# A position network with its 128 hidden channels sorted by sign: four keys a group, three partial sums added by one vector instruction and two accumulating transfers

## The chip, the cores and the metric

The kernel runs on one core of one Trainium2 chip. The metric is the device time of one execution in microseconds. Engines are called by their names in the profile: PE (matrix multiplication), PEld (PE's weight loads), DVE (vector), ACT (activation), POOL and SP (here mostly issuers of transfers), and the DMA engines behind the queues.

## The reference, cut to what matters

Four layers run one after the other on an image of 2 x 512 x 32 x 32. The change lies in the first, a deformable attention with 8 heads in each of 2 images, 1024 queries and 64 sampled keys. Each score gets a bias from a small network over the signed logarithm of the distance between query and key:

```python
pos = grid_q[:, :, None, :] - grid_kv[:, None, :, :]     # 16 heads x 1024 queries x 64 keys x 2
bias = jnp.sign(pos) * jnp.log1p(jnp.abs(pos))
bias = jax.nn.relu(bias @ cpb_w1 + cpb_b1)               # 2 -> 128
bias = jax.nn.relu(bias @ cpb_w2 + cpb_b2)               # 128 -> 128
bias = (bias @ cpb_w3 + cpb_b3)                          # 128 -> 1
sim = jnp.einsum('bhid,bhjd->bhij', qh, kh) + bias
attn = jax.nn.softmax(sim, axis=-1)
```

All data are float32. The rest of layer 0 (output projection with residual, MLP) and layers 1 to 3 are not edited.

## The kernel before, in words

`queries_keys_values` is the opening stage. It loads x into the tile `x_all`, makes q (kept padded in the tile `room`, as `q_pad`), runs the offset network (a depthwise convolution shared by PE, ACT and DVE, a gelu, a tanh), samples the keys and values, and leaves `kbd`, the keys in block form, and `val`.

`biased_scores` is the position network and more than half of the kernel. It loops over 8 head pairs p and, in each, over j = 0, 2, ... 30. Each step handles four groups t, and a group is two keys of one head (t // 2 chooses the head, t % 2 the half of its 64 keys). For one group:

- `hidden` makes one tile of 128 channels x 1024 queries for each key: an addition of two broadcast tables on DVE (L868, out of the `ab` tiles that `first_layer` loads by SP, L520, and scales on ACT, L533), then relu, in place, on ACT (L877) or, three times in sixteen, on DVE (L875). There are six such tiles.
- `second_layer` multiplies by the 128 x 128 weight in two halves of 64 channels. PE works in four column strips of 32, so that four matrix multiplications run side by side (L888). A half goes into one `ph` tile of two PSUM banks (three such tiles): strips 0 and 1 belong to the first key, 2 and 3 to the second.
- ACT evicts both halves with relu: `lo` (L898) with its bias, `hi` (L900) with a bias and a scale, the size of the last weight. DVE adds `lo` times a signed weight into `hi` (L901). This sum of 128 rows holds two keys of 64 rows each.
- `last_layer` (L909) multiplies four such sums (one j) by a 0/+1/-1 pattern into the `sim` tile (two PSUM banks), adding two keys of each group's 64 rows. It is placed one step later, behind the second group of the next j.

```python
lo = lows.tile([128, HW], F32, name="lo", tag="lo")
nc.scalar.activation(lo, phs[0], AF.Relu, bias=b2_lo)
hi = highs.tile([128, HW], F32, name="hi", tag="hi")
nc.scalar.activation(hi, phs[1], AF.Relu, bias=size_b, scale=size)
nc.vector.scalar_tensor_tensor(hi, lo, low_w, hi, ALU.mult, ALU.add)
```

At j = 16 of each p, `scores` adds q times k into the same `sim` banks (L921), and at the next p's start `store` copies `sim` to `simT` (L931). From p = 4 on, steps of the first image's softmax are woven in. At the last p, `q_pad` is no longer needed behind j = 16, and `load_weights` fills that tile with `out_w` and `mlp_w1` by SP (L321, L322). The output projection (L1055, L1067) and the MLP (L1127, L1116) follow. `Mlp` loads `mlp_w2` by SP (L217).

In float32 each matrix multiplication of the program shows up as two PE instructions. PE's order is the program's own (`manual_schedule`); the other engines' order comes from a scheduler, and each engine works its queue off in order. The compiler puts a semaphore wait where a tile is reused.

Of the kernel before, what the change touches and what calls it, by code (L numbers as in the profile page):

```python
# [16 lines left out]
B = 2  # L17
# [55 lines left out]
def constants():  # L73
    p = np.arange(128)
    px, py = (p % 32).astype(np.float32), (p // 32).astype(np.float32)
    neg_y = np.stack([-(py + 4.0 * c) for c in range(8)], axis=1).astype(np.float32)
    j = np.arange(64)
    gx, gy = (j % 8).astype(np.float32), (j // 8).astype(np.float32)

    gj = np.stack([gx, gy]).reshape(2, 1, 4, 16).repeat(16, axis=1)  # L80
    gj = gj.transpose(2, 0, 1, 3).reshape(128, 16)
    line = (2.0 * np.arange(32, dtype=np.float32) / np.float32(31) - 1.0).astype(np.float32)
    groups = np.zeros((128, 128), np.float32)
    for g in range(8):
        groups[16 * g : 16 * g + 16, 16 * g : 16 * g + 16] = 1.0 / 16

    y, x = np.divmod(np.arange(HW), 32)
    taps = np.zeros((HW, 9, 2), np.float32)
    for k in range(9):
        taps[:, k, 0] = y + k // 3 - 1  # L90
        taps[:, k, 1] = x + k % 3 - 1
    taps = taps.reshape(8, 128, 18).transpose(1, 0, 2).reshape(128, 144)
    parts = [
        ("ident", np.eye(128, dtype=np.float32)),
        ("groups", groups),
        ("minus", np.broadcast_to(np.array([0.0, -1.0], np.float32), (128, 2))),
        ("neg_xh", -px[:, None] - np.float32(0.5)),
        ("neg_yh", neg_y - np.float32(0.5)),
        ("gx", np.broadcast_to(gx, (128, 64))),
        ("gy", np.broadcast_to(gy, (128, 64))),  # L100
        ("gj", gj),
        ("line", np.broadcast_to(line, (128, 32))),
    ]
    packed, at = _pack(parts)
    return packed, at, taps


def layouts(i):
# [10 lines left out]
    for name in ("cpb_b2", "cpb_w3"):  # L119

        halves = np.asarray(i["L0_conv_" + name]).reshape(2, 64, 1)
        parts.append((name, np.concatenate([_twice(halves[0]), _twice(halves[1])], axis=1)))
# [20 lines left out]
    cst, cst_at, taps = constants()  # L143
# [8 lines left out]
    for h in range(2):  # L152
# [17 lines left out]
        "w2": np.asarray(i["L0_conv_cpb_w2"]),  # L170
# [24 lines left out]
class Net:  # L195
# [11 lines left out]
    def load_x(self):  # L207
        for b in range(B):
            for cc in range(CC):
                queue = (self.nc.sync, self.nc.gpsimd)[cc % 2]  # L210
                rows = slice(128 * cc, 128 * cc + 128)
                queue.dma_start(out=self.x[:, b, cc, :], in_=self.ins["x"][b, rows, :])
# [64 lines left out]
def layers(net, out):  # L277
# [12 lines left out]
    with ExitStack() as later:  # L290
# [12 lines left out]
        with ExitStack() as l0a:  # L303
# [8 lines left out]
            w2 = keys.tile([128, 128], F32, name="w2_t", tag="w2")  # L312
            first = net.pool(l0a, "cpb_ab", 4)
            parts = queries_keys_values(net, bn, simT, q_flat, q_pad, kbd, val, feat, first)
            nc.sync.dma_start(out=w2, in_=net.ins["w2"])

            def load_weights():
                t = new_room()
                w1 = t[:, : 4 * 2048].rearrange("p (k m) -> p k m", m=2048)
                out_w = t[:, 4 * 2048 :].rearrange("p (k m) -> p k m", m=C)  # L320
                nc.sync.dma_start(out=out_w, in_=net.ins["out_w"])  # L321
                nc.sync.dma_start(out=w1, in_=net.ins["mlp_w1"])  # L322
                return w1, out_w

            w1, out_w = biased_scores(
                net, q_pad, kbd, feat, w2, simT, first, parts, load_weights
            )
# [290 lines left out]
def queries_keys_values(net, bn, simT, q_flat, q_pad, kbd, val, feat, first):  # L618
# [5 lines left out]
    with ExitStack() as ctx:  # L624
# [3 lines left out]
        net.load_x()  # L628
# [11 lines left out]
        with ExitStack() as part:  # L640
# [33 lines left out]

            pd = bank("pd")
# [6 lines left out]
            nc.scalar.activation(g, g, AF.Gelu, bias=net.vec("odw_b"))  # L682

        with ExitStack() as part:
# [61 lines left out]

            for gt, name in grids:
# [58 lines left out]
            for w, out, factor in ((kw, kbd, 64**-0.5), (vw, val, 1.0)):  # L806
                for q in range(2):
# [15 lines left out]
                    )  # L823
    return done


def biased_scores(net, q_pad, kbd, feat, w2, simT, first, parts, load_weights):
# [12 lines left out]
    with ExitStack() as ctx:  # L840
        small = net.pool(ctx, "cpb_w", 1)
        hid1 = net.pool(ctx, "cpb_h1", 6)
        lows = net.pool(ctx, "cpb_lo", 2)
        highs = net.pool(ctx, "cpb_hi", 6)
        ps_h = net.psum(ctx, "cpb_ps_h", 3)
        ps_sim = net.psum(ctx, "cpb_ps_sim", 1)
        w3_lo, w3_hi = net.vec("cpb_w3", 0), net.vec("cpb_w3", 1)
        b2_lo, b2_hi = net.vec("cpb_b2", 0), net.vec("cpb_b2", 1)
        sign = small.tile([128, 1], F32, name="sign", tag="sign")
        nc.vector.tensor_scalar(sign, w3_hi, 0.0, 2.0, ALU.is_ge, ALU.mult)  # L850
        nc.vector.tensor_scalar(sign, sign, 1.0, None, ALU.subtract)
        size = small.tile([128, 1], F32, name="size", tag="size")
        nc.vector.tensor_tensor(size, w3_hi, sign, ALU.mult)
        size_b = small.tile([128, 1], F32, name="size_b", tag="size_b")
        nc.vector.tensor_tensor(size_b, size, b2_hi, ALU.mult)
        low_w = small.tile([128, 1], F32, name="low_w", tag="low_w")
        nc.vector.tensor_tensor(low_w, w3_lo, sign, ALU.mult)

        w3 = small.tile([128, 62], F32, name="w3", tag="w3")
        nc.vector.memset(w3, 0.0)  # L860
        nc.vector.tensor_copy(w3[0:64, 30:31], sign[0:64, :])
        nc.vector.tensor_copy(w3[64:128, 31:32], sign[64:128, :])

        def hidden(i, j, on_vector):
            at_x, at_y = parts[i, j % 32 // 16]
            k = 16 * (j // 32) + j % 16
            h1 = hid1.tile([128, HW], F32, name="h1", tag="h1")
            nc.vector.tensor_tensor(  # L868
                h1.rearrange("p (y x) -> p y x", x=32),
                at_x[:, k : k + 1, :].to_broadcast([128, 32, 32]),  # L870
                at_y[:, k, :].unsqueeze(2).to_broadcast([128, 32, 32]),
# [6 lines left out]
            return h1  # L878

        def second_layer(pair):  # L880

            phs = []
            for k in range(2):
                ph = ps_h.tile([128, HW], F32, name="ph", tag="ph")
                for n in range(2):
                    for t in range(4):
                        c0 = 64 * k + 32 * (t % 2)
                        nc.tensor.matmul(  # L888
                            ph[32 * t : 32 * t + 32, half(n)],
                            lhsT=w2[:, c0 : c0 + 32],  # L890
                            rhs=pair[t // 2][:, half(n)],
                            start=True,
                            stop=True,
                            skip_group_check=True,
                        )
                phs.append(ph)
            lo = lows.tile([128, HW], F32, name="lo", tag="lo")
            nc.scalar.activation(lo, phs[0], AF.Relu, bias=b2_lo)  # L898
            hi = highs.tile([128, HW], F32, name="hi", tag="hi")
            nc.scalar.activation(hi, phs[1], AF.Relu, bias=size_b, scale=size)  # L900
            nc.vector.scalar_tensor_tensor(hi, lo, low_w, hi, ALU.mult, ALU.add)  # L901
            return hi

        def last_layer(sim, j, sums):


            for n in range(2):
                for t in range(4):
                    nc.tensor.matmul(  # L909
                        sim[32 * t : 32 * t + 32, half(n)],  # L910
                        lhsT=w3[:, 30 - j : 62 - j],
                        rhs=sums[t][:, half(n)],
                        start=(j == 0),
                        stop=(j == 30),
                        skip_group_check=True,
                    )

        def scores(p, sim):
            for n in range(2):
                for t in range(2):  # L920
                    nc.tensor.matmul(  # L921
                        sim[64 * t : 64 * t + 64, half(n)].rearrange("p (y x) -> p y x", x=32),
                        lhsT=kbd[:, p, 64 * t : 64 * t + 64],
                        rhs=q_pad[:, p, 1 + 16 * n : 17 + 16 * n, 1:33],
                        start=False,
                        stop=False,
# [3 lines left out]
        def store(p, sim):  # L930
            nc.vector.tensor_scalar(simT[:, p, :], sim, net.vec("cpb_b3"), None, ALU.add)  # L931
# [16 lines left out]
        hidden_done = 0  # L948
        for p, j in [(p, j) for p in range(NP) for j in range(0, 32, 2)]:
            if j % 16 == 8:  # L950
                nxt = 2 * p + j // 16 + 1
                if nxt < 2 * NP:
                    parts.update(list(first_layer(net, first, feat, *divmod(nxt, 2)))[-1])
            sums = []
            for t in range(4):
                pair = []
                for k in range(2):
                    key = j + 32 * (t % 2) + k
                    pair.append(hidden(2 * p + t // 2, key, hidden_done % 16 in (3, 8, 13)))
                    hidden_done += 1  # L960
                sums.append(second_layer(pair))
                if t == 1 and pending is not None:
# [5 lines left out]
            elif j == 16:  # L968
                scores(p, sim)
                if p == NP - 1:  # L970
                    weights = load_weights()
            pending = (p, j, sums)
            if p >= CC and j % 8 == 4:
                next(beside, None)
        for _ in beside:
# [3 lines left out]
        return weights  # L979
# [1184 lines left out]
```

## Time and profile before

| | |
|---|---|
| three runs | 3830.58, 3833.95, 3833.63 us; median 3833.63 us |
| profiled execution | span 3835.8 us from the first to the last instruction; no other time is given for it, and it stands 2.2 us above the median of the runs |
| PE | 3739.0 us busy (97%), granted clock 0.992 in the mean |
| DVE, ACT | 2765.5 us (72%), 2566.4 us (67%) |
| POOL | 189.1 us (5%) |
| position network, from the first L888 to the last L909 | 86.6 to 2122.2 us |
| transfers | 168.57 MB, 44 GB/s in the mean |

How to read it: a group's line gives the source line, engine, operation, the tiles written and read, and how often; then the total busy time in us and the mean of one in ns; then the idle time before it and who ended it. Busy times of instructions that overlap are counted once in a total, so that a total can be less than count times mean. PE's matrix multiplications are pipelined and four strips overlap, so there the total divided by the count, not the mean, is the pace.

### The profile page before, as it was taken

To read this page: it belongs to the slowest core of one execution; us is meant where nothing else is said; L and a number is where in the kernel's file an instruction comes from. 1 tells how busy PE (TensorE), PEld (TensorE's weight loads), DVE (VectorE), ACT (ScalarE), POOL (GpSimd) and SP (SyncE) were. 2 spreads that over 40 slices of the span, in tenths; PEclk is the share of its full clock that TensorE was granted. 3 is DMA by queue.
4 is the path that set the end of the run, shared out by engine and by line. 5 is a ranking of instruction groups with operands and counts; after the bars stand their busy time and mean duration, and the time that the engine had idled before them with its cause. 6 is when DMAs were issued, how large, how long until landed. Compare 5 with 4: busy or idle time off the path is not lost. (4 is left out here: it accounts for less than half of the span.)

```text
span 3835.8 us, 59384 instructions
## 1 busy us (share of the span) xinstructions
PE 3739.0 (97%) x25356; PEld 1487.3 (39%) x25356; DVE 2765.5 (72%) x3242; ACT 2566.4 (67%) x2941; POOL 189.1 (5%) x180
## 2 busy tenths in 40 slices
PE   7999999999999999999999999999979999899999
PEld 4532222223222322232323444444434544455555
DVE  6999999999999999999999210411475472566565
ACT  7999999999999999999999221211123243345544
POOL 0000000000000000000000000000261150000000
PEclk9999999999999999999999999999999999999999
DMA  3000000000000000000000100112455481000000
GB/s 111 1 23 23 23 1 23 23 23 12 12 23 23 12 12 23 23 12 12 23 23 34 61 0 0 40 61 77 143 185 173 140 276 42 1 12 1 1 20 25
DMA packets 54459, 168.57 MB, mean 44 GB/s; under 512 B 4804, under 2 KB 10436, under 8 KB 51252
## 3 DMA queue, kind: packets, MB, share of 16 engines
q1 hardware_dynamic: 31556, 83.77, 6.2%
q0 software_dynamic: 21776, 79.14, 6.2%
q8 instruction: 200, 3.28, 0.4%
q10 hardware_dynamic: 864, 1.86, 0.2%
q14 instruction: 63, 0.52, 0.0%
HBM read 156.11 MB, written 8.65 MB: 43 GB/s over the span
## 5 line engine op out<-in xcount | busy, mean ns | idle before, releaser
L888 PE MATMUL ph<-h,w_t 128*32 128x512 f32 x16384 | 1808.0, 593 | 15.7 <-ACT lo L898 6.5
L868 DVE TENSOR_TENSOR h<-ab 128x1024 f32<-128x1024 f32 x1024 | 1206.0, 1219 | 67.2 <-PE ph L888 66.2
L888 PEld LDWEIGHTS ph<-h,w_t 128*32 128x32 f32 x16384 | 547.6, 110 | 1239.9 <-issue 1017.2
L877 ACT ACTIVATE h<-h 128x1024 f32<-128x1024 f32 x832 | 872.1, 1067 | 45.6 <-DVE h L868 42.9
L901 DVE SCALAR_TENSOR_TENSOR hi<-lo,low_w,hi 128x1024 f32<-128x1024 f32 x512 | 654.8, 1279 | 31.6 <-ACT hi L900 30.3
L900 ACT ACTIVATE hi<-ph,size_b,size 128x1024 f32<-128x1024 f32 x512 | 621.3, 1214 | 16.7 <-PE ph L888 12.5
L898 ACT ACTIVATE lo<-ph,vec_t 128x1024 f32<-128x1024 f32 x512 | 571.8, 1117 | 5.8 <-PE ph L888 5.4
L2086 ACT ACTIVATE e<-pl,m 128x1024 f32<-128x1024 f32 x128 | 143.6, 1122 | 228.9 <-DVE m L2078 228.9
L1567 PE MATMUL po<-fold,turned 128*128 128x512 f32 x576 | 266.1, 606 | 3.2 <-DVE dfacc L1575 2.9
L2078 DVE TENSOR_REDUCE m<-pl 128x1 f32<-128x1024 f32 x128 | 150.7, 1219 | 147.2 <-PE pl L1988 147.2
L1135 ACT ACTIVATE h<-ph,vec_t 128x512 f32<-128x512 f32 x64 | 44.0, 687 | 312.0 <-PE ph L1127 311.5
L909 PE MATMUL sim<-hi,w 128*32 128x512 f32 x2048 | 251.0, 592 | 0.0
L1127 PE MATMUL ph<-xn,room 128*128 128x512 f32 x512 | 230.9, 594 | 0.0
L1116 PE MATMUL acc<-h,mlp_w_t 128*128 128x512 f32 x512 | 229.8, 592 | 0.0
L1514 DVE SCALAR_TENSOR_TENSOR sum<-got,wts,sum 128x256 f32<-128x256 f32 x432 | 184.4, 478 | 48.8 <-ACT sum L1510 46.4
L1490 POOL DMA_INDIRECT got<-table,idx x144 | 175.0, 1215 | 554.9 <-DVE sum L1514 268.0
L2040 PE MATMUL pt<-cst_t,e 128*128 128x128 f32 x1024 | 149.3, 279 | 6.6 <-ACT aT L2051 4.0
L2040 PEld LDWEIGHTS pt<-cst_t,e 128*128 128x128 f32 x1024 | 118.6, 142 | 93.6 <-issue 61.3
L1567 PEld LDWEIGHTS po<-fold,turned 128*128 128x128 f32 x576 | 106.6, 195 | 112.4 <-issue 107.4
L1116 PEld LDWEIGHTS acc<-h,mlp_w_t 128*128 128x128 f32 x512 | 97.3, 190 | 122.5 <-issue 122.0
L1127 PEld LDWEIGHTS ph<-xn,room 128*128 128x128 f32 x512 | 96.6, 191 | 117.7 <-issue 117.1
L1541 ACT COPY turned<-pt 128x512 f32<-128x512 f32 x72 | 41.9, 582 | 143.8 <-PE pt L1535 143.6
(250 smaller groups left out, 2711.6 us busy)
## 6 DMA issues: line engine op xcount, KB each, us to landing
ab<-feat_d SPq DMA_DIRECT2D x64, 512.0 KB, 4.0
room<-in_dc_w_dram SPq DMA_DIRECT2D x9, 1024.0 KB, 4.8
dc_w_t<-in_dc_w_dram SPq DMA_DIRECT2D x5, 1024.0 KB, 5.3
room<-in_mlp_w_dram SPq DMA_DIRECT2D x1, 4096.0 KB, 15.6
mlp_w_t<-in_mlp_w_dram SPq DMA_DIRECT2D x1, 4096.0 KB, 12.5
dc_w_t<-in_dc_w_dram SPq DMA_DIRECT2D x8, 512.0 KB, 5.0
w_qkv_t<-in_w_qkv_dram SPq DMA_DIRECT2D x3, 1024.0 KB, 8.6
out_dram<-x_all SPq DMA_DIRECT2D x12, 256.0 KB, 2.0
```

The source lines that it names most:

```text
L868: nc.vector.tensor_tensor(h1.rearrange("p (y x) -> p y x", x=32), at_x[:, k : k + 1, :].to_broadcast([128, 32, 32]), at_y[:, k, :].unsquee ...
L877: nc.scalar.activation(h1, h1, AF.Relu)
L888: nc.tensor.matmul(ph[32 * t : 32 * t + 32, half(n)], lhsT=w2[:, c0 : c0 + 32], rhs=pair[t // 2][:, half(n)], start=True, stop=True, skip_ ...
L898: nc.scalar.activation(lo, phs[0], AF.Relu, bias=b2_lo)
L900: nc.scalar.activation(hi, phs[1], AF.Relu, bias=size_b, scale=size)
L901: nc.vector.scalar_tensor_tensor(hi, lo, low_w, hi, ALU.mult, ALU.add)
L909: nc.tensor.matmul(sim[32 * t : 32 * t + 32, half(n)], lhsT=w3[:, 30 - j : 62 - j], rhs=sums[t][:, half(n)], start=(j == 0), stop=(j == 30 ...
L1116: nc.tensor.matmul(accs[oc], lhsT=self.w2[:, m, 128 * oc : 128 * oc + 128], rhs=hs[m], start=(m == 0), stop=(m == 15),)
L1127: nc.tensor.matmul(ph, lhsT=self.w1[:, k, 128 * m : 128 * m + 128], rhs=xn[:, k, :], start=(k == 0), stop=(k == CC - 1),)
L1514: nc.vector.scalar_tensor_tensor(t[:, q, :], g[:, s, :], w, t[:, q, :], ALU.mult, ALU.add)
L1567: nc.tensor.matmul(self.out, lhsT=turned[:, at : at + 128], rhs=self.folded.w[k][:, i, :], start=(k == 0 and i == 0), stop=(k == 8 and i = ...
L2040: nc.tensor.transpose(pt[:, 128 * c : 128 * c + 128], e[:, 128 * k : 128 * k + 128], ident)
```

## The change

The 128 channels of the second layer are sorted on the chip by the sign of their last weight, so that one lane of 32 rows has the same sign in the last three quarters; the first quarter may have lanes whose sign differs. The size of each last weight is multiplied into the second layer's weights and bias. A group is then four keys, one for each strip of 32 rows, and the 128 channels are done in four quarters. `Order` makes the sorted weights in the opening stage (`ranks`, `places`, `put`: small instructions on one column, two loads, seven small matrix multiplications).

- `hidden` makes two keys in one instruction of 128 x 2048. Its tiles are nine pairs: five in `room`, whose `q_pad` is no longer needed, and four in `x_all`. Seven relus in sixteen are on DVE.
- `second_layer`: four quarters into four `ph` tiles; ACT evicts all four with relu and a bias. DVE adds the first to the second (`lo`, one buffer). The third and fourth (`r2`, two buffers; `r3`, three) are added by transfers with `accum_op=ALU.add`, issued by POOL from SBUF to SBUF; the fourth's is issued one group later, behind the next group's third.
- `last_layer` runs for every fourth key instead of every second, behind the third group of the next step. Eight buffers hold the totals, as against six.
- q times k is done for all p at the end of the opening stage and copied to `simT` by DVE and ACT; `store` adds to it.
- x is loaded again by SP: the first image and `out_w` at the last p's j = 24, when three of the nine pairs are given up, the second image at the end; `mlp_w1` comes in four parts at the end.

```diff
+    def put(self, bank):
+        net, nc = self.net, self.net.nc
+        pw, pb = bank("pw2"), bank("pb2")
+        nc.tensor.matmul(pw[:, :128].rearrange("p (q l) -> p q l", l=32),
+            lhsT=self.turned, rhs=self.spread[:, :, 0, :], start=True, stop=True)
...
+            order.places(ranks)
...
+            order.put(bank)
...
+            for p in range(NP):
+                for n in range(2):
+                    pq = bank("pqk")
+                    for t in range(2):
+                        nc.tensor.matmul(
+                            pq[64 * t : 64 * t + 64, :].rearrange("p (y x) -> p y x", x=32),
+                            lhsT=kbd[:, p, 64 * t : 64 * t + 64],
+                            rhs=q_pad[:, p, 1 + 16 * n : 17 + 16 * n, 1:33],
...
+                    (nc.vector.tensor_copy, nc.scalar.copy)[n](simT[:, p, half(n)], pq)
...
-        hid1 = net.pool(ctx, "cpb_h1", 6)
-        lows = net.pool(ctx, "cpb_lo", 2)
-        highs = net.pool(ctx, "cpb_hi", 6)
+        lows = net.pool(ctx, "cpb_lo", 1)
+        thirds = net.pool(ctx, "cpb_r2", 2)
+        fourths = net.pool(ctx, "cpb_r3", 3)
+        highs = net.pool(ctx, "cpb_hi", 8)
...
             nc.vector.tensor_tensor(
-                h1.rearrange("p (y x) -> p y x", x=32),
-                at_x[:, k : k + 1, :].to_broadcast([128, 32, 32]),
-                at_y[:, k, :].unsqueeze(2).to_broadcast([128, 32, 32]),
+                h1.rearrange("p k (y x) -> p k y x", x=32),
+                at_x[:, k : k + 2, :].unsqueeze(2).to_broadcast([128, 2, 32, 32]),
+                at_y[:, k : k + 2, :].unsqueeze(3).to_broadcast([128, 2, 32, 32]),
                 ALU.add,
             )
...
+        def quarter(quad, q):
+            ph = ps_h.tile([128, HW], F32, name="ph", tag="ph")
+            for n in range(2):
+                for t in range(4):
+                    nc.tensor.matmul(
+                        ph[32 * t : 32 * t + 32, half(n)],
+                        lhsT=order.w2[:, 32 * q : 32 * q + 32],
+                        rhs=quad[t][:, half(n)],
...
+        def second_layer(quad, late):
+            r0 = rectified(quarter(quad, 0), 0, lows, "lo")
+            total = rectified(quarter(quad, 1), 1, highs, "hi")
+            nc.vector.scalar_tensor_tensor(total, r0, order.low, total, ALU.mult, ALU.add)
+            r2 = rectified(quarter(quad, 2), 2, thirds, "r2")
+            r3 = rectified(quarter(quad, 3), 3, fourths, "r3")
+            nc.gpsimd.dma_start(out=total, in_=r2, accum_op=ALU.add)
+            flush(late)
+            late.append((total, r3))
+            return total
+
+        def flush(late):
+            for total, more in late:
+                nc.gpsimd.dma_start(out=total, in_=more, accum_op=ALU.add)
+            late.clear()
...
         def store(p, sim):
-            nc.vector.tensor_scalar(simT[:, p, :], sim, net.vec("cpb_b3"), None, ALU.add)
+            nc.vector.scalar_tensor_tensor(
+                simT[:, p, :], sim, net.vec("cpb_b3"), simT[:, p, :], ALU.add, ALU.add
+            )
...
-        for p, j in [(p, j) for p in range(NP) for j in range(0, 32, 2)]:
+        rooms = room.rearrange("p (n k i) -> p n k i", k=2, i=HW)
+        tiles = [rooms[:, n] for n in range(5)]
+        tiles += [net.x[:, b, c : c + 2, :] for b in range(B) for c in range(0, CC, 2)]
+        slots = list(range(9))
+        for p, j in [(p, j) for p in range(NP) for j in range(0, 32, 4)]:
...
+            if (p, j) == (NP - 1, 24):
+                slots = [at for at in slots if at not in (4, 5, 6)]
+                load_out()
+                net.load_x(0, [nc.sync])
...
-                    pair.append(hidden(2 * p + t // 2, key, hidden_done % 16 in (3, 8, 13)))
+                    on_vector = pairs_done * 7 % 16 < 7
+                    quad += hidden(2 * p + t // 2, key, tiles[slots[0]], on_vector)
...
-                if t == 1 and pending is not None:
+                if t == 2 and pending is not None:
                     last_layer(sim, *pending[1:])
...
+        net.load_x(1, [nc.sync])
+        flush(late)
```

## The prediction

> **What bounds the kernel now.** I read first the slices of the profile's page, to find the stage, then the costliest groups of instructions, then the busy time of each engine in stretches of the stage, then the rows of transfers that POOL issues, and last the order of time around the stage's two ends.
>
> ```profile
> PE   7999999999999999999999999999979999899999
> DVE  6999999999999999999999210411475472566565
> ACT  7999999999999999999999221211123243345544
> DMA  3000000000000000000000100112455481000000
> ```
>
> For the first 22 of 40 slices PE, DVE and ACT are all above 90%, while the DMA engines do next to nothing. That is the position network, from 86.6 to 2122.2 us: 2035.6 us, or 7.95 us for each of 256 sets of four keys.
>
> ```profile
> L888 PE MATMUL ph<-h,w_t 128*32 128x512 f32 x16384 | 1808.0, 593 | 15.7 <-ACT lo L898 6.5
> L868 DVE TENSOR_TENSOR h<-ab 128x1024 f32<-128x1024 f32 x1024 | 1206.0, 1219 | 67.2 <-PE ph L888 66.2
> L877 ACT ACTIVATE h<-h 128x1024 f32<-128x1024 f32 x832 | 872.1, 1067 | 45.6 <-DVE h L868 42.9
> L901 DVE SCALAR_TENSOR_TENSOR hi<-lo,low_w,hi 128x1024 f32<-128x1024 f32 x512 | 654.8, 1279 | 31.6 <-ACT hi L900 30.3
> L900 ACT ACTIVATE hi<-ph,size_b,size 128x1024 f32<-128x1024 f32 x512 | 621.3, 1214 | 16.7 <-PE ph L888 12.5
> L898 ACT ACTIVATE lo<-ph,vec_t 128x1024 f32<-128x1024 f32 x512 | 571.8, 1117 | 5.8 <-PE ph L888 5.4
> L909 PE MATMUL sim<-hi,w 128*32 128x512 f32 x2048 | 251.0, 592 | 0.0
> ```
>
> PE waits 15.7 us in all for anyone; DVE and ACT mostly wait for PE or for each other. The stretch 300 to 600 us settles it (PE, PEld, DVE, ACT, POOL busy, then PE's clock, DMA share, GB/s):
>
> ```profile
> 300.00:600.00 300.00, 298.18 (x2756) 88.18 (x2752) 284.77 (x259) 292.56 (x287) 0.00 (x0) 1.00 0.07 22
> ```
>
> PE is the bound at 99.4%, at full clock. ACT at 97.5% and DVE at 94.9% are close behind, so a gain on PE alone would be lost to ACT within 2%; all three have to come down together. The pace is 300 / 2756 = 0.1089 us for one matrix multiplication.
>
> **The change part by part.** *PE.* The second layer keeps its 16384 instructions. The last layer has one sum for four keys instead of two: 1024 of 2048 fall away, 1024 x 0.1089 = 111.5 us. The 64 of q times k (L921, 15.5 us busy) move ahead of the stage. The stage's PE pace becomes (2035.6 - 111.5 - 15.5) / 256 = 7.46 us a group of four keys.
>
> *ACT.* A group has four evictions with a bias, like L898: 4 x 1.117 = 4.47. Relu of a pair: L898 against its 512-wide kin L1135 (0.687) gives 0.43 for 512 elements, so 1.067 + 0.86 = 1.93; nine sixteenths of two pairs are 1.125 x 1.93 = 2.17. The tables cost 64 x 1.219 / 256 = 0.30. Sum 6.94 by means; neighbours overlap by some 5% in the rows of before, so about 6.5 of 7.46. *DVE.* Two additions of a pair (1.219 at 1024 and 0.689 at 512 give 1.06 for 1024 more, so 2.28): 4.56. Relu of a pair (0.686 at 1024, 0.42 at 512, so 1.21) 0.875 times: 1.06. One L901: 1.28. `store` 0.04. Sum 6.94, about 6.6 with overlap. Both fall from 95% and more to about 88% of PE's time. That cover is what makes PE's gain count: if it were gone, DVE without overlap would still be under 7.46.
>
> *The transfers.* Here lies the risk. Nothing in the trace accumulates. The nearest rows are the gathers of layer 1, which POOL issues too, 512 KB each; the view of transfers in the stretch 2460 to 3170 us gives the software queue's packets, MB and share of the engines, and the median us to landing:
>
> ```profile
> q0 software_dynamic: 20896, 76.03, 32.3%
> ...
> got<-table,idx POOLq DMA_INDIRECT x144, 5.3
> ```
>
> So 76.03 MB took 0.323 x 710 = 229 us of all sixteen engines, 332 GB/s, 1.58 us for 512 KB, with 5.3 us from issue to landing and, by the median of L1490, 0.94 us of POOL. Lower bound of an accumulating one: a copy's 1.58 us. Upper bound: it lands before the next begins, 5.3 us. I take 3.2 us, twice a copy, because the sum has two sources to read; it is nearer to the copy's row, because gathers overlap in flight (58 of them, 307 us of landing times, lie between 2700 and 2900 us). Two a group are 6.4 us, the `ab` loads (64 x 1.58 / 256) 0.4: 6.8 of 7.46 us, hidden with a tenth to spare. The limit is (7.46 - 0.39) / 2 = 3.53 us; above it the transfers set the pace, and at 3.75 us the whole gain is gone.
>
> The Trainium skill ("Collectives: The Full Stack", section "The bandwidth ceiling: the fold count and why AG ≠ RS ≠ AR") holds that adding in the transfer is slow through its two source reads and not through the addition, and gives 31 GB/s an engine halved. By that rule sixteen engines would add 250 GB/s, an estimate from that page, 2.1 us a transfer, and the sum would be the same, with more room; no run here shows it.
>
> The added waits: ACT's `r2` waits for the transfer two groups back, `r3` for the one three back that was issued a group late, and behind them stand all evictions, so PE. With 5.3 + 1.6 us to land, `r2`'s is done some 7 us after issue, and ACT needs it after 14.9; the totals must be ready 2 groups and more after the last issue. So nothing waits as long as the rate holds. POOL's order is third of this group, then fourth of the last; 2 x 0.94 us of POOL is a quarter of a group.
>
> DVE and POOL can also hold each other up. L650, a `tensor_scalar` of 128x1024, takes 0.80 us seven times, and 1.72 us the one time that POOL's memsets L634 and L635 run beside it, at 6.3 us. No row shows the same beside an issue of POOL. If every one of the 224 relus on DVE were held for one issue, 0.94 us, DVE would go from 6.6 to 7.4 us a group, just short of PE. The Trainium skill ("SBUF — State Buffer", section "Who interferes with whom") makes it a rule, and one that speaks against this change: a vector instruction that uses both of DVE's port pairs and POOL's descriptor writing lock each other out for their whole length.
>
> *Opening stage.* 32 small DVE instructions come between the convolution's L591, which runs back to back there. Such ones (L853 to L862) start 0.07 to 0.16 us apart: 2.2 to 5.1, I take 3.5. The ten behind the gelu fit into DVE's wait of 3.18 us for `nt`. Moving q times k puts 15.5 us ahead of the first L888, but PE stood idle 3.4 + 0.5 us there for the first `hidden`, and that is now filled: -3.9. The 16 copies (0.69, 0.58 us) run on two engines beside it. The small matrix multiplications lie in PE's idle 6.3 us before L788. Emptying PSUM for the next pool: +1.
>
> *End of the stage.* Before, L900, L901 and L909 followed the last L888; DVE's part was 1.28 us:
>
> ```profile
> 2117.11 1.21 ACT L900 ACTIVATE hi<-ph,size_b,size 128x1024 f32<-128x1024 f32 x1 [0.60 <-PE ph L888]
> ...
> 2118.34 1.28 DVE L901 SCALAR_TENSOR_TENSOR hi<-lo,low_w,hi 128x1024 f32<-128x1024 f32 x1 [2.15 <-ACT hi L900]
> ```
>
> Now two transfers stand there one behind the other, each 3.9 (the fastest gather) to 7 us, the first starting one quarter, 1.74 us, earlier: 7.8 to 14, less 1.74 and 1.28, so +4.8 to +11, and SP's reloads run at that moment: +9. The reloads themselves: `mlp_w1` landed in 15.6 us before, and the first L1127 comes at 2155.9, 38 us after the last L888; the second image is needed later still, and `mlp_w2` (12.5 us) behind it at 2162.4. 10 MB at 332 GB/s are 32 us, so 6 us of cover remain; without it the MLP would start late by as much. At j = 24 `out_w` and an image, 3 MB, hold the transfers up by 9 us once, less than the 7.5 us of slack plus what the buffers give.
>
> *Sum.* -111.5 + 3.5 - 3.9 + 1 + 9 = -102, and I expect PE's 0.6% of idling in the stage, 12 us, to halve with the other engines' slack: -6. 3835.8 - 108 = 3728 in the profile's terms; the span is 2.2 us over the median, so 3725.
>
> **The rivals.** *The transfers pace the stage* (slower). Place: POOL's queue and the sixteen engines; it decides from 3.53 us on. If an addition costs three passes (two reads, one write, 4.75 us), a group is 2 x 4.75 + 0.4 = 9.9 us, and the time 3725 + 256 x 2.44 = 4350 us; at 5.3 us, 4630. For it: no row of accumulation, and a margin of a tenth. Against it: the copy's 1.58 us lies far below.
>
> *Just at the edge.* Transfers of 3.6 to 3.75 us, or DVE held by POOL without its overlap (6.94 + 0.82 = 7.76 us): 20 to 90 us back, 3745 to 3815.
>
> *It does not do what it says.* If PE's pace were set by ACT's chain rather than by its own count, taking 1024 away would bring little; PE's wait of 15.7 us speaks against it. Time: about 3833.
>
> **How the numbers follow.** Forecast 0.66, with its own range 3690 to 3760: all ends at their best (-111.5 - 12 - 3.9 + 2.2 + 4.8, and PE at the 0.1075 us that L909's rows of 16 show) to all at their worst and 20 us of the reloads uncovered. Edge 0.12, faster still. No change 0.03. Paced by transfers 0.19. A difference of 0.2%, 7.7 us, is about what a measurement of this kernel can tell. Faster 0.78, same 0.03, slower 0.19. The range runs from 3690 to 3850; left out are nearly all of the slower case and a little at the bottom.
>
> **What would show it.** Right: L909's successor x1024, PE above 98% in the stage at about 7.4 us a group, DMA share there 0.8 to 0.95, DVE and ACT below 92%, 4 to 11 us of PE idle at the stage's end. Wrong: PE's idle time ended by ACT evictions that in turn wait for DMA, a DMA share of 1 with POOL waiting for its own transfers, or a relu on DVE far above 1.2 us.

## The result, and the profile after

| | before | after |
|---|---|---|
| median (range) | 3833.1 us (3830.6 to 3834.0, 4 runs) | 3993.6 us (3985.4 to 3997.4, 4 runs) |
| profiled execution's span | 3835.8 us | 3989.8 us |
| PE, DVE, ACT, POOL busy | 97%, 72%, 67%, 5% | 92%, 65%, 57%, 16% |

The changed kernel is slower by 160 us: ratio 1.0414, 95% interval 1.0400 to 1.0429. The forecast of 3725 us, and its range, were wrong.

The slices of the changed kernel's page:

```profile
PE   7998899989899999899998799999988999999999
DVE  7987788778778888788887211320366374466665
ACT  7887777777787777777876321021113233245544
DMA  3577777776777677767777700012345473000000
```

In the position network PE has fallen from solid nines to a mixture with eights, and DVE and ACT to seven and eight tenths. DMA stands at seven tenths, neither idle nor full. No engine is the bound. The costliest groups say what they wait for:

```profile
L1017 PE MATMUL ph<-room,w_t 128*32 128x512 f32 x9184 | 1255.8, 597 | 108.9 <-ACT r L1029 78.8
L1017 PE MATMUL ph<-x_all,w_t 128*32 128x512 f32 x7200 | 1030.1, 596 | 84.7 <-ACT r L1029 67.1
L1029 ACT ACTIVATE r<-ph,bias 128x1024 f32<-128x1024 f32 x512 | 550.5, 1110 | 409.9 <-DMA hi<-r 392.2
...
L1046 POOL DMA_DIRECT2D hi<-r x256 | 219.6, 858 | 1697.1 <-DVE hi L1036 438.4
L1039 POOL DMA_DIRECT2D hi<-r x256 | 307.1, 1200 | 80.8 <-ACT r L1029 78.2
```

PE waits 193.6 us, 145.9 of them for evictions of `r2` and `r3`, and these in turn wait 392 us for transfers (`hi<-r`) to give their buffers back. I call the third quarter's transfer A2 (L1039) and the fourth's A3 (L1046). Of POOL's two rows, A3's has nearly all of the idle time in front of it, 1697 us against 81. The stretch 300 to 600 us (PE, PEld, DVE, ACT, POOL busy, PE's clock, DMA share, GB/s), and then the view of transfers in it (packets, MB, share of the engines; below it KB each):

```profile
300.00:600.00 300.00, 264.50 (x2380) 73.33 (x2376) 235.82 (x136) 226.78 (x189) 61.03 (x70) 1.00 0.72 141
```

```profile
q0 software_dynamic: 10126, 36.83, 65.6%
...
hi<-r POOLq DMA_DIRECT2D x70, 512.0 KB
```

70 transfers took 0.656 x 300 = 197 us of all sixteen engines, **2.81 us each**, less than the 3.2 that I took and than my limit of 3.53. So their price alone doesn't explain the loss. POOL's order of time does:

```profile
1003.53 0.85 POOL L1046 DMA_DIRECT2D hi<-r  x1 [10.99 <-DVE x_all L1008]
1004.07 1.21 POOL L1039 DMA_DIRECT2D hi<-r  x1
1011.22 0.86 POOL L1046 DMA_DIRECT2D hi<-r  x1 [5.94 <-ACT hi L1029]
1011.75 1.21 POOL L1039 DMA_DIRECT2D hi<-r  x1
1020.14 0.85 POOL L1046 DMA_DIRECT2D hi<-r  x1 [7.18 <-DVE hi L1036]
```

A3 goes first and A2 0.54 us behind it. Then POOL stands for 6 to 11 us, and a waiting A3 opens the next pair. The brackets name whatever ended last by the profile, often an instruction that writes nothing an A3 reads (`x_all`, for one); 279.7 us, in 44 waits, are put down to the transfers themselves. The engines work in bursts between:

```profile
1004.80:1009.90 5.10, 3.31 (x32) 0.59 (x24) 0.00 (x0) 5.10 (x5) 0.47 (x1) 1.00 1.04 197
1009.90:1012.50 2.60, 2.27 (x24) 0.78 (x28) 1.28 (x2) 2.54 (x4) 1.28 (x2) 1.00 0.13 24
```

5.1 us with all of them at work without pause (share 1.04), then 2.6 nearly empty. The trace doesn't say which group an A3 belongs to, since buffer numbers are left out, but the instruction list of the built kernel does. POOL's queue holds:

```
L1039 hi_892<-r2_904
L1046 hi_892<-r3_915
L1039 hi_942<-r2_954
L1046 hi_942<-r3_965
```

The source writes A2 of a group and then A3 of the group before (`flush(late)`). The scheduler, free to order POOL, put A3 right behind the A2 of its *own* group. The first rows of the stage show the same: when the first A3 comes, one A2 alone has gone, and the A3 waits for a transfer.

```profile
118.46 0.91 POOL L1039 DMA_DIRECT2D hi<-r  x1 [75.40 <-ACT r L1029]
123.59 0.87 POOL L1046 DMA_DIRECT2D hi<-r  x1 [4.23 <-DMA hi<-r]
124.89 0.86 POOL L1039 DMA_DIRECT2D hi<-r  x1 [0.43 <-issue]
```

A3 must wait for A2 to land, since both add into one tile, and it waits at the head of POOL's queue, so the next group's A2 stands behind it. That makes one round a group. The shorter of the two rounds shown above, from the A3 at 1003.53 to the one at 1011.22, takes 7.7 us: 0.5 between the two issues, 2 x 2.81 of data, and a remainder of some 1.6 (an estimate) for the way from issue to start and from landing to the next issue. The next one takes 8.9. Over the stage the median of 255 rounds is 8.1 us, and the 28 in which loads of the `ab` tiles are asked for take 9.8 in the mean. The stage, from PE's first L1017 at 107.0 to its last at 2246.7, took 8.36 us a group where PE needs under 7.46.

### The profile page after: what moved, and what is told of

Same layout as the page of the kernel before. It is cut to its first block, busy times and chain, and to the rows that moved or that the text cites. A ratio compares the mean times of both kernels' runs of the same rounds, so it can differ in the third digit from the quotient of the medians.

```text
span 3989.8 us, 57248 instructions
## 1 busy us (share of the span) xinstructions
PE 3688.4 (92%) x24346; PEld 1430.2 (36%) x24346; DVE 2584.3 (65%) x2562; ACT 2265.8 (57%) x2406; POOL 638.7 (16%) x692
## 5 line engine op out<-in xcount | busy, mean ns | idle before, releaser
L1017 PE MATMUL ph<-room,w_t 128*32 128x512 f32 x9184 | 1255.8, 597 | 108.9 <-ACT r L1029 78.8
L1017 PE MATMUL ph<-x_all,w_t 128*32 128x512 f32 x7200 | 1030.1, 596 | 84.7 <-ACT r L1029 67.1
L1029 ACT ACTIVATE r<-ph,bias 128x1024 f32<-128x1024 f32 x512 | 550.5, 1110 | 409.9 <-DMA hi<-r 392.2
L1001 DVE TENSOR_TENSOR room<-ab 128x2048 f32<-128x2048 f32 x287 | 646.9, 2285 | 7.3 <-PE ph L1017 7.1
L1017 PEld LDWEIGHTS ph<-room,w_t 128*32 128x32 f32 x9184 | 340.3, 110 | 835.6 <-issue 549.5
L1036 DVE SCALAR_TENSOR_TENSOR hi<-lo,low,hi 128x1024 f32<-128x1024 f32 x256 | 328.5, 1283 | 392.2 <-ACT hi L1029 391.9
L1001 DVE TENSOR_TENSOR x_all<-ab 128x2048 f32<-128x2048 f32 x225 | 507.7, 2285 | 6.9 <-PE ph L1017 6.8
L1017 PEld LDWEIGHTS ph<-x_all,w_t 128*32 128x32 f32 x7200 | 274.4, 110 | 655.2 <-issue 428.1
L1046 POOL DMA_DIRECT2D hi<-r x256 | 219.6, 858 | 1697.1 <-DVE hi L1036 438.4
L1039 POOL DMA_DIRECT2D hi<-r x256 | 307.1, 1200 | 80.8 <-ACT r L1029 78.2
L1010 ACT ACTIVATE room<-room 128x2048 f32<-128x2048 f32 x163 | 311.7, 1912 | 11.2 <-DVE room L1001 10.6
L1029 ACT ACTIVATE lo<-ph,bias 128x1024 f32<-128x1024 f32 x256 | 285.1, 1114 | 50.2 <-PE ph L1017 49.1
L1029 ACT ACTIVATE hi<-ph,bias 128x1024 f32<-128x1024 f32 x256 | 285.3, 1114 | 13.6 <-PE ph L1017 13.1
L1010 ACT ACTIVATE x_all<-x_all 128x2048 f32<-128x2048 f32 x125 | 239.0, 1912 | 4.7 <-DVE x_all L1001 4.4
```

Source lines behind the costliest of these rows:

```text
L1001: nc.vector.tensor_tensor(h1.rearrange("p k (y x) -> p k y x", x=32), at_x[:, k : k + 2, :].unsqueeze(2).to_broadcast([128, 2, 32, 32]), a ...
L1010: nc.scalar.activation(h1, h1, AF.Relu)
L1017: nc.tensor.matmul(ph[32 * t : 32 * t + 32, half(n)], lhsT=order.w2[:, 32 * q : 32 * q + 32], rhs=quad[t][:, half(n)], start=True, stop=Tr ...
L1029: nc.scalar.activation(t, ph, AF.Relu, bias=order.bias[:, q : q + 1])
L1036: nc.vector.scalar_tensor_tensor(total, r0, order.low, total, ALU.mult, ALU.add)
L1039: nc.gpsimd.dma_start(out=total, in_=r2, accum_op=ALU.add)
```

## The experiments

In kernels that put POOL in order the source lines are two higher (L1031 for L1029, L1041 and L1048 for A2 and A3). Ratios are to the kernel before, in the same set.

**First set: order, buffers, bytes, addition.**

```diff
-l0a.enter_context(net.tc.manual_schedule(engines={mybir.EngineType.PE}))
+l0a.enter_context(net.tc.manual_schedule(engines={mybir.EngineType.PE, mybir.EngineType.Pool}))
```

> Edit: POOL also follows the written order in the stage, so that A2 of a group (the third quarter's transfer) is issued ahead of A3 of the group before; nothing else changes. Order theory (POOL's built queue puts A3 of a group right behind its own A2, so one round of issue, start, data and landing is paid for each group, 8.1 to 8.5 us against PE's 7.46): the groups fall back to PE's pace, 256 x (8.4 - 7.5) = 230 us are gone, about 3763 us, with 3745 to 3790 as its bounds; PE's busy share in the window 300 to 600 us rises from 88% to 98% or more. Rate rival (two transfers of 2.81 us and their start and landing fill the DMA engines' time whatever the order): 3960 to 4000 us, and DMA bursts still follow each other with the same gaps. Buffer rival (two r2 buffers stall ACT): no change either, since the buffers are as they were.

Measured: 3850.1 us (3848.7 to 3854.7), ratio 1.0052 [1.0035, 1.0069]. POOL's first rows in the stage now have two A2 ahead of the first A3:

```profile
116.07 0.91 POOL L1041 DMA_DIRECT2D hi<-r  x1 [73.00 <-ACT r L1031]
122.52 0.86 POOL L1041 DMA_DIRECT2D hi<-r  x1 [5.54 <-DVE hi L1038]
123.07 1.20 POOL L1048 DMA_DIRECT2D hi<-r  x1
```

143 us are gone, so the order is a cause and the rate rival falls. But 230 were expected, PE is busy 281 of the 300 us from 300 on and not 98%, and the kernel is still no faster than before.

```diff
-thirds = net.pool(ctx, "cpb_r2", 2)
-fourths = net.pool(ctx, "cpb_r3", 3)
+thirds = net.pool(ctx, "cpb_r2", 3)
+fourths = net.pool(ctx, "cpb_r3", 2)
```

> Edit: three r2 buffers and two r3 buffers in place of two and three, POOL's queue as in the changed kernel. Buffer rival (ACT's third-quarter eviction waits for a buffer that the transfer two groups back still reads; that is where the trace puts ACT's 392 us of idle time): most of 240 us is gone, 3760 to 3850 us. Order theory (ACT's wait is only the place where POOL's round shows): 3980 to 4000 us, no change, and the wait moves to another instruction.

Measured: 3995.8 us (3988.6 to 4005.8), ratio 1.0423 [1.0405, 1.0440]: no change. ACT's wait (473 us here, at the same evictions) shows where POOL's round is felt, and a buffer more for `r2`, at `r3`'s cost, does not help. More buffers in all were not tried.

```diff
-nc.gpsimd.dma_start(out=total, in_=r2, accum_op=ALU.add)
+nc.gpsimd.dma_start(out=total[:, :512], in_=r2[:, :512], accum_op=ALU.add)
```

and the same for `r3`:

> Edit: both transfers of a group carry columns 0 to 511 only, so half of the additions are left out; POOL's queue as in the changed kernel. Order theory with a round made of bytes: the round of 8.1 us loses 2 x 1.4 = 2.8 us and becomes 5.3, below PE's 7.46, so 3750 to 3790 us. Latency rival (the round is mostly fixed start and landing, the bytes count little): the round stays over 7.46 us, 3880 us or more.

Measured: 3731.2 us, ratio 0.9736 [0.9720, 0.9752].

```diff
-nc.gpsimd.dma_start(out=total, in_=r2, accum_op=ALU.add)
+nc.gpsimd.dma_start(out=total, in_=r2)
```

and the same for `r3`:

> Edit: the two transfers of a group copy instead of adding, so two of the three additions are left out; POOL's queue as in the changed kernel. Order theory with the accumulation's price in it: a copy of this size takes about 1.6 of the engines' us against 2.81, the round falls from 8.1 to 5.6 us, below PE's 7.46: 3750 to 3790 us. Rival (an accumulating transfer costs no more than a copy from SBUF to SBUF, 2.8 us each): 3970 to 4000 us.

Measured: 3732.0 us, ratio 0.9736 [0.9720, 0.9752]. Both came out below the bounds expected. The software queue's row between 300 and 600 us, first of the half-width run (82 transfers), then of the copies (82):

```profile
q0 software_dynamic: 11885, 21.66, 42.2%
```

```profile
q0 software_dynamic: 11819, 43.00, 35.8%
```

A half-width addition takes 0.422 x 300 / 82 = 1.54 us of the engines, a full copy 1.31, against 2.81 for a full addition. By the sum above the round is then some 5 us, an estimate. PE is busy 299 of the 300 us in both runs and sets the pace; the scheduler's bad order costs nothing. So neither order nor price acts alone: a serial round of two additions is just longer than PE's group.

**What was left.** The run in POOL's written order is 118 us above the copies. In it, ACT's order of time shows a new wait, for the next `ab` tiles, which ACT weighs at L535:

```profile
313.22 1.11 ACT L1031 ACTIVATE r<-ph,bias 128x1024 f32<-128x1024 f32 x1
317.90 1.24 ACT L535 ACTIVATE ab<-ab,vec_t 128x1024 f32<-128x1024 f32 x1 [3.56 <-DMA ab<-feat_d]
319.04 1.09 ACT L1031 ACTIVATE r<-ph,bias 128x1024 f32<-128x1024 f32 x1
```

The same kernel's view of the tile `ab`, idle time of ACT (us, times) and landing times:

```profile
  DMA ab<-feat_d: 117.1, 34
...
DMA to landing us min/median/max: 3.6/8.9/11.8
```

Before, the median was 4.0 us and ACT waited 0.4 us in all. The additions now use the same engines, and a load takes twice as long (with half widths and with copies in their place 4.7 and 4.5 us). The evictions stand behind L535 in ACT's queue.

**Second set: the loads.**

```diff
-if j % 16 == 8:
-    nxt = 2 * p + j // 16 + 1
-    if nxt < 2 * NP:
-        parts.update(list(first_layer(net, first, feat, *divmod(nxt, 2)))[-1])
+nxt = 2 * p + j // 16 + 1
+if j % 16 == 4 and nxt < 2 * NP:
+    weigh = first_layer(net, first, feat, *divmod(nxt, 2))
+    parts.update(next(weigh))
+if j % 16 == 12 and nxt < 2 * NP:
+    next(weigh)
```

> Edit: POOL in the written order as in the first experiment, and the loads of the next ab tiles asked of SP one quad earlier with their weighing on ACT one quad later. Load theory (what is left of the first experiment over PE's pace is ACT's queue held up by ab tiles: 117.1 us in 34 waits, their landing 8.9 us in the median against 4.0 us before, because the accumulating transfers fill the same engines): the 117 us go, 3850 - 117 = 3733 us, 3725 to 3750 as its bounds, and ACT's waits for ab are near nothing. Rate rival (0.77 of the DMA engines in use makes every transfer late, the ab waits being only one face of it): 3800 to 3850 us.

Measured: 3856.1 us (3850.5 to 3859.6), ratio 1.0054 [1.0039, 1.0070].

> Edit: only the ab loads earlier and their weighing later; POOL's queue as in the changed kernel (A3 of a group behind its own A2). Order theory (the round of a pair sets the pace; ACT waits for ab there only 4.3 us in 13 waits): 3975 to 4000 us, no change over 15 us. Load theory as the whole cause: at most 3880 us.

Measured: 3988.9 us, ratio 1.0402 [1.0386, 1.0418]. Neither run tests the theory. In the built queues ACT's L535 stands behind the same groups with and without the edit (11, 13, 27, 29, ...), and ACT waited 125.6 us for `ab` in the first of them. The scheduler put the weighing at the same place both times; by what rule, these runs don't show. I had made the same mistake again: the source was edited and the order not read. The two runs stand as repeats.

```diff
-slots = list(range(9))
+slots = [5, 6, 7, 8, 0, 1, 2, 3, 4]      # first pairs in x's bytes
...
+if by_vector:                            # last quad, second to fourth group
+    nc.vector.tensor_tensor(total, total, r2, ALU.add)
+    flush(late)
+    nc.vector.tensor_tensor(total, total, r3, ALU.add)
```

with POOL's order and the edit above:

> Edit: POOL in the written order and the ab loads early, and two more: the first pairs of the stage use x's bytes, which no longer have a reader, ahead of the room tiles whose bytes the last products of the position scores still read (PE's gap of 5.8 us at the stage's start); and in the last quad the additions of groups two to four are made by DVE (six of about 1.2 us) rather than by transfers. Theory: from the run with order and loads, about 3733, less some 5 us at the opening and 12 to 20 us at the end (in the first experiment PE's last quarter ended at 2112 us and the last product at 2138, with 13 us of waits for transfers; the additions by DVE need two times 1.3 us after the last eviction): 3713 us, 3700 to 3725. Rival (the gaps are only exchanged for other waits, as the first pairs then wait for DVE's evictions of the position scores and the rows after the stage wait for reloads): 3728 to 3740.

Measured: 3831.3 us (3827.2 to 3836.0), ratio 0.9996 [0.9987, 1.0005]. The two repairs, at the stage's opening and at its end, are worth 19 to 25 us against the runs without them; ACT's wait for `ab` stays (126.5 us), as the load edit did nothing.

**Third set: the weighing held back.** The loads' place as in the second set, and each weighing tied behind an eviction:

```diff
+if j % 16 == 8 and nxt < 2 * NP:
+    ab = parts[2 * (nxt // 2) + t // 2, nxt % 2][t % 2]
+    bias = net.vec("cpb_b1") if t % 2 == 0 else 0.0
+    with net.tc.issue_after(evicted[0].ins):
+        nc.scalar.activation(ab, ab, AF.Identity, bias=bias, scale=net.vec("cpb_w1", t % 2))
```

Here `evicted[0]` is the group's `r3` eviction. In the built queue the weighing now stands behind the groups 25 to 28 where it stood behind 11 and 13.

> Edit: POOL in the written order, and the weighing of the next ab tiles on ACT (L535's operation) held behind the third-layer evictions of the groups 12 to 14 places further on; the loads themselves go when their tiles come free, as before. The two runs with earlier loads moved no instruction on ACT (the scheduler had put the weighing right behind the load in either case), so they said nothing about ACT's wait. Load theory (ACT's queue stands still for ab tiles 117.1 us, landing 8.9 us): those waits vanish, about 3853 - 117 = 3736 us, 3725 to 3760 as bounds, PE's busy share in the windows 98% or more. Rate rival (the transfers are late in themselves and the ab wait only shows it): 3835 to 3860 us, with the waits moved to ACT's third-quarter evictions.

Measured: 3726.0 us (3724.4 to 3729.2), ratio 0.9720 [0.9705, 0.9735]. The load theory holds. The rows of PE and the stretch 300 to 600 us:

```profile
L1019 PE MATMUL ph<-room,w_t 128*32 128x512 f32 x9184 | 1213.7, 593 | 6.7 <-DVE room L1010 5.8
L1019 PE MATMUL ph<-x_all,w_t 128*32 128x512 f32 x7200 | 997.3, 592 | 0.5 <-ACT r L1031 0.5
```

```profile
300.00:600.00 300.00, 300.00 (x2800) 91.35 (x2796) 278.72 (x162) 266.95 (x222) 72.91 (x84) 1.00 0.84 166
```

PE waits 7.2 us for the operands and banks of the second layer's products in the whole stage, and the DMA engines are busier (0.84) than in the slow kernel (0.72). The loads land no sooner than in the first experiment (median 9.1 us); only nobody waits for them: ACT's wait for `ab` is 0.2 us.

> Edit: the run with all repairs (POOL's order, first pairs in x's bytes, the last three groups added by DVE: 3831 us), and the weighing of ab held back as in the other run of this set. Load theory: 3831 - 117 = 3714 us, 3700 to 3735 as bounds, the fastest of all kernels here. Rate rival: 3815 to 3835 us.

Measured: 3705.9 us (3704.1 to 3706.9), ratio 0.9664 [0.9651, 0.9677]. This version beats both kernels: 129 us under the one before, 288 under the changed one.

**Fourth set: the parts apart.**

> Edit: only ACT's weighing of the ab tiles held back; POOL's queue as in the changed kernel (A3 of a group right behind its own A2). Order theory (the round of a pair alone sets the pace there, ACT waits for ab 4.3 us in all): 3970 to 3995 us, no gain over 15 us. Load theory as a cause of its own (the two causes add, 117 us each way): 3994 - 117 = 3877 us or less.

Measured: 3983.9 us, ratio 1.0390 [1.0374, 1.0406]. Without POOL's order the late weighing is worth 10 us at most (the time ranges of the two kernels overlap), behind it 124. The causes don't add: a second wait is hidden under the first and shows when the first is gone.

> Edit: the kernel with POOL's order and the late weighing (3726 us), and only the first pairs of the stage moved to x's bytes. Theory: PE's gap of 5.8 us at the stage's opening falls to under 1, as in the run with all repairs: 3721 us, 3719 to 3723; the remaining 15 us to that run (3706 us) are then the last groups' additions by DVE. Rival (the opening's gap only moves on to the next groups, all of the 20 us are the end's): 3725 to 3728 us.

Measured: 3723.0 us (3715.1 to 3723.9), ratio 0.9704 [0.9690, 0.9717], 3 us below the run without it. Their time ranges lie half a us apart, so these times alone don't settle it. PE's order of time shows the gap gone; first the kernel with order and late weighing, then this one:

```profile
88.93 14.02 PE L964 MATMUL pqk<-room,kbd 128*64 128x512 f32 x64
108.78 3.62 PE L1019 MATMUL ph<-room,w_t 128*32 128x512 f32 x14 [5.82 <-DVE room L1010]
```

```profile
87.39 14.02 PE L964 MATMUL pqk<-room,kbd 128*64 128x512 f32 x64
102.09 10.50 PE L1019 MATMUL ph<-x_all,w_t 128*32 128x512 f32 x95 [0.68 <-ACT simT L972]
```

From the first row to the second it is 14.7 us against 19.9, but the stage behind took 1882.9 us against 1880.0: about half came back there, as the rival had it, and with one profile of each this is not settled. The kernel with all repairs (3706 us) differs from this one by the last groups' additions alone, so these are worth 17 us. PE's products into `sim` after the last quarter, in the kernel with order and late weighing, then in the one with all repairs:

```profile
1990.35 1.04 PE L1056 MATMUL sim<-hi,w 128*32 128x512 f32 x2 [0.58 <-DMA hi<-r]
2000.40 1.92 PE L1056 MATMUL sim<-hi,w 128*32 128x512 f32 x2 [9.00 <-DMA hi<-r]
...
2008.06 1.04 PE L1056 MATMUL sim<-hi,w 128*32 128x512 f32 x2 [2.03 <-DMA hi<-r]
2010.48 3.37 PE L1056 MATMUL sim<-hi,w 128*32 128x512 f32 x10 [1.38 <-DMA hi<-r]
```

```profile
1988.94 1.06 PE L1061 MATMUL sim<-hi,w 128*32 128x512 f32 x6
...
1991.21 1.91 PE L1061 MATMUL sim<-hi,w 128*32 128x512 f32 x10
```

The last transfers cost 13 us of waits there, and DVE, idle at that moment, saves them.

## Why the prediction was wrong

The parts of the sum, us, from the profiled spans. The stage is from PE's first product of the second layer to its last.

| | predicted | after | order and late weighing |
|---|---|---|---|
| until the stage | 102.7 | 107.0 | 108.8 |
| stage | 1897.5 | 2139.7 | 1880.0 |
| until the last product into `sim` | 14.1 | 31.3 | 25.1 |
| the rest | 1713.6 | 1711.8 | 1708.7 |
| span | 3727.9 | 3989.8 | 3722.6 |

- **The step that failed** is "POOL's order is third of this group, then fourth of the last". It was read from the source, for an engine whose order the scheduler makes. With the built order, two transfers a group are not 5.6 us of throughput under a limit of 7.07 but a chain of 7.7 us or more. My limit of 3.53 us for one was worked out for a free queue; in the built one it lies near (7.46 - 0.5 - 1.6) / 2 = 2.7 us, an estimate from the rows above, and the additions took 2.81. The stage came out 242 us too long; mending the order gave back 143 us of the whole time by itself, and 258 between the two kernels with the weighing held back (3983.9 and 3726.0).
- **A second step was missing.** I priced the `ab` loads in DMA time (0.4 us a group), not in what their doubled landing time does at the head of ACT's queue. It was worth 124 us as soon as POOL's order was mended.
- The rival "the transfers pace the stage" had the right place, POOL's queue, and the right sign, but not the mechanism: its condition and time (from 3.53 us, 4350 us) were wrong, since it reasoned with the engines' rate too. The sign named beforehand did appear: PE's idle time ended by ACT's evictions that wait for DMA. The DMA share of 1 did not, outside single bursts; the mean was 0.72.
- **Opening**, 4.3 us off: I had PE's gap filled, but the first additions write into `room`, whose bytes the last product of q and k still reads (the wait of 5.8 us for DVE in the row of the fourth set). **End**, 17 us off: +9 predicted, +26 measured (31.3 against 5.1 before); I priced one group's two transfers, but in the changed kernel PE waited there three times in a row for transfers (10.4, 5.7 and 3.0 us), those of the groups before being late too; the share of SP's reloads in it was not tried apart. With POOL in order it is still +20.
- **What held**: the saving on PE and the prices of the instructions. The pair's addition took 2285 ns (2.28 us predicted), ACT's relu 1912 (1.93), DVE's 1226 in the median (1.21). With both waits gone the kernel ran in 3726 us. That it meets the forecast of 3725 is in part luck: the stage was 17 us quicker than predicted (PE took 2800 products between 300 and 600 us, where the forecast kept the 2756 of before) and the two ends 17 longer.
- DVE held up by POOL, the case at the edge, is not seen: the changed kernel's 124 relus in `room` took 1215, 1226 and 1229 ns (least, median, most), with 512 issues on POOL in the stage. The reverse is seen: a POOL issue that met a relu of DVE before its last 0.1 us ended only behind it. Four issues in the changed kernel took 1.44 to 2.22 us, where the others took at most 1.25, and each ended 0.08 to 0.13 us after the relu beside it; four of 512 cost nothing that can be told. Of the others 245 lie wholly within a pair addition of DVE (L1001) and show nothing of the kind. The Trainium skill ("SBUF — State Buffer", section "Who interferes with whom") has the two lock each other out for a whole instruction; on POOL's side these rows agree. The half-width run has far more such issues, for example this one, which ends at 143.98 us, the relu at 143.86:

```profile
142.50 1.48 POOL L1046 DMA_DIRECT2D hi<-r  x1 [2.93 <-issue]
142.63 1.23 DVE L1008 TENSOR_SCALAR x_all<-x_all 128x2048 f32<-128x2048 f32 x1
```

- The Trainium skill ("Collectives: The Full Stack", section "The bandwidth ceiling: the fold count and why AG ≠ RS ≠ AR") puts the price of adding in the transfer down to a second source read and halves the rate. An addition here took 2.81 / 1.31 = 2.1 times a copy, which agrees. The 2.1 us that I estimated from its 31 GB/s an engine do not, as 512 KB in 2.81 us are 187 GB/s and not 250; the page gives that figure for rings of collectives, and carrying it over to sixteen engines was my step.
- Two slips in the working changed nothing: by the prediction's own sum, transfers of 3.6 to 3.75 us give back 33 to 110 us and not 20 to 90, and the first of the 22 slices stands at 6 to 7 tenths, not above 90%.

## What to carry to other kernels

An instruction's place on an engine that a scheduler orders has to be read from the built queue, before a wait is priced and again before an experiment's edit is believed. Two dependent transfers side by side in one in-order queue cost their whole chain, landing included, so compare that chain and not their share of the DMA engines with the bound's period. And when new transfers begin to fill the engines, loads that were there before can land later, as the `ab` loads did here: look for who waits for them at the head of a queue.

## What the runs showed of the hardware that was not expected

An addition from SBUF into SBUF of 512 KB takes 2.75 to 2.81 us of all sixteen DMA engines (2.75 in the kernel with order and late weighing: 0.769 of 300 us for 84), where a copy of the same bytes takes 1.31. Next to such additions, with 0.72 to 0.84 of the engines in use between 300 and 600 us, 512 KB loads that had landed in 4.0 us took 7.4 to 9.4 in the median; next to copies (0.43) or half-width additions (0.49) they took 4.5 and 4.7.
